# A graph layer on one core: edge features and q spans of the next pair ahead of the last node tile, span products behind the next tile, and every gather tied to one matmul

## The chip, the cores and the metric

The kernel runs on one core of a Trainium2 chip. The metric is the device time of one execution in microseconds; three executions of the kernel before took 3551.51, 3549.98 and 3547.55 us, a median of 3549.98.

A core has a matrix engine (TensorE, PE in the profile, with its weight loads shown apart as PEld), a vector engine (VectorE, DVE), a scalar engine (ScalarE, ACT), GpSimd (POOL), which here does nothing but issue gathers, and a fifth queue (SP), which here only issues transfers. Each engine works through its own queue in program order; engines wait for each other on semaphores, which an instruction raises when it ends. [...]

## The reference

One layer of message passing over 12500 nodes and 400000 edges, which are sorted by their target `dst`. All features are 32 wide, the hidden layer 64.

```python
h = jnp.maximum(_layernorm(x, axis=-1), 0.0)
...
    rol, col = (edge_index[0], edge_index[1])
    e_feat = jnp.concatenate([x[rol], x[col], edge_attr], axis=-1)
    h = jax.nn.relu(e_feat @ W1 + b1)
    v = h @ W2 + b2
    x_cand = jax.ops.segment_max(v, col, num_segments=num_nodes)
    return jnp.maximum(x_cand, x[:, -v.shape[-1]:])
x = x + _L0_gnn_ref(h, edge_index, edge_attr_32, ...)
```

Inside `_L0_gnn_ref` the argument `x` is the normalized `h`. So each edge needs the row of its source node, the row of its target node and its own 32 features; each node then takes the maximum over its edges.

## The kernel before

**Chunks.** The edges are cut into four stripes (`NS` = 4), which lie side by side on the 128 partitions, 32 features each. A stripe is cut into 196 chunks of 512 edges (`NCH`, `C`), so a chunk is 2048 edges. The main loop (L858) takes two chunks at a time, `c` and `c + 1`, and prepares the next two, `a = c + 2` and `b = c + 3`. One such pass is called an iteration here; there are 97, and the pieces under `if c:` are left out of the first.

**Layer one** adds three products into four PSUM banks `ph` (one for each stripe, the two chunks in its two halves), eight matmuls each: edge features (`edges_into`, operand `ea`), the target's part (`windows_into`; the dst order makes the targets of a chunk a short span of nodes, so `qf`, that span of the product q = h @ W1 part, is multiplied by a one-hot matrix `of`) and the source's part (`rows_into`, operand `ht`, the source rows turned so that features lie on partitions). All three go through `into_ph`, so all have line L777; they are told apart by operand. The page counts each of these matmuls as two records. ScalarE's `relu` (L802) reads the four banks into `hid`, `second_layer` (L811) multiplies by W2, and VectorE's `scan` (L819) takes the running maximum along the sorted edges.

**Source rows** come two ways. Of the 16 blocks of 128 edges in a chunk, 12 are gathered by POOL (`gather`, L181, one block of 128 rows an instruction), so 24 an iteration. The other four are picked on TensorE: `tile(c, m)` (L330) multiplies a one-hot matrix `hot` by the whole node table `hs`, held on the chip in two parts, in 14 matmuls (7 groups by 2 parts, L346); VectorE then masks the 14 candidates (`one`, L355) and reduces them to one row (`gm`, L356). A tile takes TensorE 2.9 us. In 34 chunks an extra tile `tile(b, MM)` stands for a twelfth gather (operands `hot`, `zero` and `xg` in the profile). `to_features` turns gathered rows (L372) and tile rows (L375) into `ht` on VectorE.

**Results of spans.** The iteration after, `leave_1` transposes the maxima on TensorE (L673, eight matmuls, into two banks), ScalarE and VectorE copy and split them (`so`), `leave_2` picks the last edge of each target by a matmul (L690, eight matmuls into one bank `pw`, the "span products") and copies one half on ScalarE (`wo`, L696), and `leave_3` adds the other half on VectorE (L704) and stores on SP.

**TensorE's order in one iteration**, before: edge features(c), q spans(c), rows(c), transposes, tile a1, a2, a3, second layer(c), span products, tile b0, b1, b2, b3, the extra tile where there is one, and the first tile of the chunk a + 2, called n0 below. On ScalarE the copy `wo` stands right behind the second layer, ahead of the one-hots of a + 2 (`one_hots_act`, L319 and L320).

**The order is written by hand** (`manual_schedule`): what each engine does follows the order of the Python statements, and semaphores are set where data need them. PSUM banks are handed out by `bank` from a ring of seven (`BANKS` = 7, L233): the request number k gets the bank of request k - 7 and waits for its last reader.

**Gathers held back.** A gather needs nothing but its indices and a free buffer. `HELD` holds it until a named matmul has ended: key is the gather's place among the 24, value how many iterations before the one that uses its rows, and which matmul. `passes` notes the matmuls under a name, `hold` (L220) notes the waits. Names like `a1-` and `a1` are the middle and the end of a tile, `ea`, `ht`, `tr`, `lv` the end of a group. Twenty of the 24 are held; 7, 11, 18 and 23 are not. `SOON` holds the third and fourth chunk's first ones.

## Time and profile before

| | |
|---|---|
| median of three executions | 3549.98 us |
| the profiled execution | 3553.86 us |
| its span, first to last instruction | 3552.1 us |
| mean granted TensorE clock | 0.942 of full speed |
| TensorE busy | 3301.4 us, 93% |
| VectorE, POOL, ScalarE busy | 63%, 62%, 44% |
| DMA, mean over the span | 64 GB/s |

All times in the profile are microseconds from the start of the span unless marked ns. A group in the page or in a list by lines reads: line, engine, operation, result <- operand, partitions x elements and type, count, then busy time, mean ns of one instruction, and how long the engine had been idle just before, with what ended most of that idle time ("issue" where the profile shows no reason). A timeline reads: start, duration, the same names, and in brackets the idle time ahead of the piece with what ended it; "remote" is a signal whose sender the profile doesn't tell. A windows line reads: stretch, its length, the busy time and count of PE, PEld, DVE, ACT and POOL, the granted clock, the DMA share and GB/s. Consecutive instructions of the same form stand in one line with their count.

### The profile page before, as it was taken

Reading aid. Unit: us, or ns where it says so; the run is one execution under the profiler, and the core shown is the slowest. Engines: PE = TensorE matmul, PEld = TensorE weight load, DVE = VectorE, ACT = ScalarE, POOL = GpSimd, SP = SyncE. Lnnn points to the kernel's source line nnn. Section 1 sums busy time; section 2 is a strip of 40 time slices with the busy share of each in tenths; the row PEclk is TensorE's granted clock in tenths of the full one; section 3 lists DMA queues with packets and bytes.
Section 4 is the critical chain, followed back from the end, with each engine's and each line's share of the span. In section 5 each row is a group of like instructions: output and inputs, shape, how many; then the busy total and the mean of one; then the engine's idle time right before and its main releaser. Section 6 shows DMA issues by size and latency. Waiting matters only on the chain. (4 is left out here: it accounts for less than half of the span.)

```text
span 3552.1 us, 55930 instructions
## 1 busy us (share of the span) xinstructions
PE 3301.4 (93%) x19141; PEld 2554.6 (72%) x19141; DVE 2230.3 (63%) x4215; ACT 1566.6 (44%) x2470; POOL 2208.2 (62%) x2337
## 2 busy tenths in 40 slices
PE   4799999999999999999999999999999999999997
PEld 3577777777777777777777767677767777777674
DVE  5466666666666666666666666665756666666665
ACT  4344444444444444444444444444444444444343
POOL 7566666666666666666666666666666666666662
PEclk8799999999999999999999999999999999999997
DMA  6322222212222222222222222222222222221222
GB/s 198 79 58 62 53 64 60 66 50 65 63 63 53 65 59 66 51 65 63 62 50 69 58 65 50 62 62 66 51 65 60 64 53 62 60 68 49 59 58 65
DMA packets 178823, 227.53 MB, mean 64 GB/s; under 512 B 109621, under 2 KB 150373, under 8 KB 165734
## 3 DMA queue, kind: packets, MB, share of 16 engines
q10 hardware_dynamic: 29828, 108.01, 9.5%
q0 software_dynamic: 74336, 38.21, 7.9%
q1 hardware_dynamic: 74370, 77.70, 7.2%
q8 instruction: 151, 2.47, 0.3%
q14 instruction: 138, 1.13, 0.1%
HBM read 212.23 MB, written 11.46 MB: 63 GB/s over the span
## 5 line engine op out<-in xcount | busy, mean ns | idle before, releaser
L181 POOL DMA_INDIRECT gh<-h_d,src_i x2291 | 2169.9, 947 | 1278.4 <-issue 520.4
L346 PE MATMUL pv<-hs,hot 128*128 128x448 f32 x10752 | 2319.5, 374 | 84.7 <-issue 76.9
L346 PEld LDWEIGHTS pv<-hs,hot 128*128 128x128 f32 x10752 | 2062.9, 194 | 293.5 <-issue 123.7
L355 DVE TENSOR_TENSOR one<-pv,mask 128x448 f32<-128x448 f32 x768 | 473.9, 617 | 1201.0 <-PE pv L346 569.5
L802 ACT ACTIVATE hid<-ph,wt 128x512 f32<-128x512 f32 x392 | 241.3, 688 | 1174.2 <-remote 439.0
L356 DVE TENSOR_REDUCE gm<-one 128x32 f32<-128x448 f32 x768 | 476.3, 620 | 26.5
L306 DVE TENSOR_TENSOR hot<-kb,consts 128x1024 fp32r<-128x1024 f16 (+1 forms) x379 | 447.5, 1199 | 0.0
L320 ACT ACTIVATE hot<-away,ones 128x512 fp32r<-128x512 f32 x582 | 421.8, 725 | 27.5 <-remote 8.5
L319 ACT ACTIVATE away<-kb,key_n 128x512 f32<-128x512 f16 x582 | 416.7, 716 | 0.0
L777 PE MATMUL ph<-ht,wt 32*64 32x512 f32 x1568 | 316.8, 679 | 44.6 <-issue 30.3
L696 ACT ACTIVATE wo<-pv 128x256 f32<-128x256 f32 x95 | 36.6, 385 | 673.8 <-PE pv L346 472.2
L819 DVE TENSOR_TENSOR_SCAN sm<-pb,sm,pv 128x512 f32<-128x512 bf16 x195 | 243.8, 1250 | 17.5 <-PE pv L690 6.0
L777 PEld LDWEIGHTS ph<-ht,wt 32*64 32x64 f32 x1568 | 83.3, 139 | 206.9 <-issue 178.1
L673 PEld LDWEIGHTS pv<-ident,sb 128*128 128x128 f32 x782 | 109.9, 171 | 137.9 <-issue 93.0
L372 DVE STREAM_TRANSPOSE ht<-gh 128x96 f32<-128x96 f32 x774 | 207.4, 269 | 1.2
L777 PE MATMUL ph<-of,qf 32*64 32x512 f32 x1552 | 172.8, 602 | 19.5 <-issue 16.8
L673 PE MATMUL pv<-ident,sb 128*128 128x128 f32 x782 | 150.4, 338 | 26.6 <-issue 20.5
L690 PEld LDWEIGHTS pv<-so,last 128*128 128x128 f32 x768 | 99.8, 189 | 95.6 <-issue 87.6
L665 ACT ACTIVATE sb<-sm,wt 128x512 f32<-128x512 f32 x196 | 134.3, 713 | 64.6 <-issue 41.0
L646 ACT ACTIVATE of<-of,ones 128x512 f32<-128x512 f32 x194 | 140.6, 725 | 6.3
L690 PE MATMUL pv<-so,last 128*128 128x256 f32 x768 | 126.2, 298 | 14.5 <-issue 12.9
L645 ACT ACTIVATE of<-db,below 128x512 f32<-128x512 int32 x194 | 137.4, 708 | 2.2 <-DMA db<-in_dst_ext 2.2
(115 smaller groups left out, 1330.4 us busy)
## 6 DMA issues: line engine op xcount, KB each, us to landing
ea<-in_edge_attr SPq DMA_DIRECT2D x49, 1024.0 KB
db<-in_dst_ext ACTq DMA_DIRECT2D x48, 1024.0 KB
gh<-h_d,src_i POOLq DMA_INDIRECT x2291
pb<-pen_d ACTq DMA_DIRECT2D x48, 512.0 KB
kb<-key_d ACTq DMA_DIRECT2D x47, 512.0 KB
top_d<-wo SPq DMA_DIRECT2D x752, 3.0 KB
qf<-q_d SPq DMA_DIRECT2D x392, 16.0 KB
q_d<-qs SPq DMA_DIRECT2D x6, 512.0 KB
```

The lines of the kernel that those rows point to most:

```text
L181: ins = nc.gpsimd.indirect_dma_start(out=parts[-1][:, i, :], out_offset=None, in_=h_d[:, :], in_offset=bass.IndirectOffsetOnAxis(ap=src_i[ ...
L306: nc.vector.tensor_tensor(hot_of(c)[:, start:stop], keys[c][:, None, :].to_broadcast([P, n, MM * P]), key_ps[:, start:stop, None].to_broad ...
L319: nc.scalar.activation(away, keys[c], AF.Square, bias=key_n[:, k:k + 1])
L320: nc.scalar.activation(hot_of(c)[:, k], away, AF.Relu, bias=ones, scale=-1.0)
L346: ins = nc.tensor.matmul(po, hot[k], hs[:, part, k].rearrange("p f a -> p (f a)"), start=(k == 0 and part == 0), stop=(k == A1 - 1 and par ...
L355: nc.vector.tensor_tensor(one, of_group, mask[:, None, :].to_broadcast([P, D, A0]), op=ALU.mult)
L356: nc.vector.tensor_reduce(row, one, axis=AX.X, op=ALU.max)
L673: passes(c // 2 + 1, "tr", nc.tensor.transpose(px[:, j, :], sb[:, j * P:(j + 1) * P], ident))
L690: ins = nc.tensor.matmul(pw[:, x % n], last[x][:, j].rearrange("p s w -> p (s w)"), sos[x][0][:, j], start=(j == 0 and x < n), stop=(j == ...
L777: ins = nc.tensor.matmul(ph[s][x * HID:(x + 1) * HID], w[g], e[g], start=start, stop=stop)
L802: nc.scalar.activation(hid[k], of, AF.Relu, bias=b1c)
L819: nc.vector.tensor_tensor_scan(found[:, :n], loaded.pop(c)[2][:, :n], pv[:, :n], -LOW if before is None else before[:, C - 1:C], op0=ALU.a ...
```

## The change

Four things change. `edges_into` and `windows_into` for the next pair are no longer called at the loop's top, but at the end of the iteration before, ahead of `tile(a + 2, 0)`. `leave_2`, with its copy `wo`, moves from behind `second_layer` to behind `tile(b, 0)`. `passes` gets an index, so that every single matmul of the groups can be named. `HELD` then holds all 24 gathers, each by one matmul (`b2.4` is the fifth of tile b2's fourteen).

TensorE's order after: rows(c), transposes, tile a1, a2, a3, second layer(c), tile b0, span products, tile b1, b2, b3, the extra tile, edge features(c + 2), q spans(c + 2), n0.

```diff
--- before.py
+++ after.py
@@ -64,11 +64,12 @@
 LATE = NCH - 8
 PIECE = 2 * A0
 GP = 3
-HELD = {0: (3, 'b1'), 1: (3, 'b2-'), 2: (3, 'b2'), 3: (3, 'b3-'), 4: (3, 'b3'), 5: (3, 'n0-'), 6: (3, 'n0'),
-        8: (2, 'ea'), 9: (2, 'ht'), 10: (2, 'tr'), 12: (2, 'a1-'), 13: (2, 'a1'), 14: (2, 'a2-'), 15: (2, 'a2'),
-        16: (2, 'a3-'), 17: (2, 'a3'), 19: (2, 'lv'), 20: (2, 'b0-'), 21: (2, 'b0'), 22: (2, 'b1-')}
+HELD = {0: (3, 'b1.13'), 1: (3, 'b2.4'), 2: (3, 'b2.10'), 3: (3, 'b3.3'), 4: (3, 'b3.11'), 5: (2, 'ea.0'),
+        6: (2, 'ea.7'), 7: (3, 'n0.4'), 8: (3, 'n0.12'), 9: (2, 'ht.1'), 10: (2, 'ht.7'), 11: (2, 'a1.0'),
+        12: (2, 'a1.4'), 13: (2, 'a1.9'), 14: (2, 'a2.0'), 15: (2, 'a2.8'), 16: (2, 'a3.2'), 17: (2, 'a3.9'),
+        18: (2, 'l2.0'), 19: (2, 'l2.4'), 20: (2, 'b0.6'), 21: (2, 'lv.0'), 22: (2, 'b1.0'), 23: (2, 'b1.8')}
 BANKS = 7
-SOON = {(3, 0): 'a0', (3, 6): 'a2', (4, 0): 'a3', (4, 6): 'b0', (5, 0): 'b1', (5, 6): 'b2'}
+SOON = {(3, 0): 'a0.13', (3, 6): 'a2.13', (4, 0): 'a3.13', (4, 6): 'b0.13', (5, 0): 'b1.13', (5, 6): 'b2.13'}
 ROUND = 12582912.0
 LOW = 1e30
 BY_ACT = range(A1 - 3, A1)
@@ -213,9 +214,9 @@
     gh = {}
     passed = {}
 
-    def passes(iteration, name, ins):
-
-        passed[iteration, name] = ins
+    def passes(iteration, name, ins, k):
+
+        passed[iteration, f"{name}.{k}"] = ins
 
     def hold(c, i, ins):
 
@@ -345,11 +346,9 @@
             for part in range(2):
                 ins = nc.tensor.matmul(po, hot[k], hs[:, part, k].rearrange("p f a -> p (f a)"),
                                  start=(k == 0 and part == 0), stop=(k == A1 - 1 and part == 1))
-            if k in (A1 // 2, A1 - 1):
-                at = "" if k == A1 - 1 else "-"
                 if m == 0 and c % 2 == 0:
-                    passes(c // 2 - 2, "n0" + at, ins)
-                passes(c // 2 - 1, "ab"[c % 2] + str(m) + at, ins)
+                    passes(c // 2 - 2, "n0", ins, 2 * k + part)
+                passes(c // 2 - 1, "ab"[c % 2] + str(m), ins, 2 * k + part)
         of_group = po.rearrange("p (f a) -> p f a", a=A0)
         one = early.tile([P, D, A0], F32, name="one", bufs=2)
         nc.vector.tensor_tensor(one, of_group, mask[:, None, :].to_broadcast([P, D, A0]), op=ALU.mult)
@@ -670,7 +669,8 @@
             px = bank("pv").rearrange("p (j q) -> p j q", j=J)
             n = blocks(c)
             for j in range(n):
-                passes(c // 2 + 1, "tr", nc.tensor.transpose(px[:, j, :], sb[:, j * P:(j + 1) * P], ident))
+                ins = nc.tensor.transpose(px[:, j, :], sb[:, j * P:(j + 1) * P], ident)
+                passes(c // 2 + 1, "tr", ins, c % 2 * J + j)
             so = pool.tile([P, J, 2, P], F32R, name="so", bufs=2)
             nc.scalar.activation(so[:, :n, 0], px[:, :n], AF.Copy)
             return so, px
@@ -690,7 +690,7 @@
                     ins = nc.tensor.matmul(pw[:, x % n], last[x][:, j].rearrange("p s w -> p (s w)"),
                                            sos[x][0][:, j], start=(j == 0 and x < n),
                                            stop=(j == blocks(c + x) - 1 and x >= 2 - n))
-            passes(c // 2 + 1, "lv", ins)
+                    passes(c // 2 + 1, "lv", ins, x * J + j)
             wo = pool.tile([P, 2, P], F32, name="wo", bufs=2)
             if c < NCH - 6:
                 nc.scalar.activation(wo, pw[:, :, 0], AF.Copy)
@@ -770,27 +770,27 @@
 
         sent = {}
 
-        def into_ph(ph, pairs, start, stop):
+        def into_ph(c, name, ph, pairs, start, stop):
             for s in range(NS):
                 g = slice(s * D, (s + 1) * D)
                 for x, (w, e) in enumerate(pairs):
                     ins = nc.tensor.matmul(ph[s][x * HID:(x + 1) * HID], w[g], e[g], start=start, stop=stop)
-            return ins
+                    passes(c // 2, name, ins, 2 * s + x)
 
         def edges_into(c):
 
             ph = banks[c] = [bank("ph") for s in range(NS)]
-            passes(c // 2, "ea", into_ph(ph, [(w1c, loaded[c + x][0]) for x in range(2)], True, False))
+            into_ph(c, "ea", ph, [(w1c, loaded[c + x][0]) for x in range(2)], True, False)
             return ph
 
         def windows_into(c, ph):
             of = [ofs.pop(c + x) for x in range(2)]
             q = fetched.pop(c // 2)
-            into_ph(ph, [(q[:, x], of[x]) for x in range(2)], False, False)
+            into_ph(c, "of", ph, [(q[:, x], of[x]) for x in range(2)], False, False)
 
         def rows_into(c, ph):
             ht = [hts.pop(c + x).rearrange("p k e -> p (k e)") for x in range(2)]
-            passes(c // 2, "ht", into_ph(ph, [(w1a, ht[x]) for x in range(2)], False, True))
+            into_ph(c, "ht", ph, [(w1a, ht[x]) for x in range(2)], False, True)
 
         def relu(c):
 
@@ -809,7 +809,7 @@
                 for x in range(2):
                     g = slice(x * HID, (x + 1) * HID)
                     ins = nc.tensor.matmul(pv[x][s * D:(s + 1) * D], w2x[g], hid[s][g], start=True, stop=True)
-            passes(c // 2, "l2", ins)
+                    passes(c // 2, "l2", ins, 2 * s + x)
             return pv
 
         def scan(c, pv, before):
@@ -857,9 +857,6 @@
         windows_into(0, ph)
         for c in range(0, NCH - 4, 2):
             a, b = c + 2, c + 3
-            if c:
-                ph = edges_into(c)
-                windows_into(c, ph)
             rows_into(c, ph)
             if c % LOAD:
                 load_edges(c + LOAD // 2 + AHEAD)
@@ -895,8 +892,6 @@
                 tile(a + 2, 0)
             pv = second_layer(c, hid)
             if c:
-                pw = leave_2(c - 2, so, last)
-            if c:
                 one_hots_act(a + 2)
             load_keys(a + KEYS)
             load_key_x(b + 2)
@@ -910,6 +905,7 @@
             sms = [scan(c, pv[0], sm)]
             if c:
                 tile(b, 0)
+                pw = leave_2(c - 2, so, last)
                 to_features(b, 0)
             sms.append(scan(c + 1, pv[1], sms[0]))
             sm = sms[1]
@@ -954,13 +950,11 @@
             tile(b, MM)
             to_features(b, 3)
             to_features(b, J)
+            ph = edges_into(c + 2)
+            windows_into(c + 2, ph)
             if a + 2 < NCH - 2:
                 if c:
                     tile(a + 2, 0)
-            else:
-                ph = edges_into(c + 2)
-                windows_into(c + 2, ph)
-            if a + 2 < NCH - 2:
                 to_features(a + 2, 0)
             if c == (NB - 1) * BLOCK + 2:
                 bp = bank("pv")[:, 0:1]
```

## The prediction

> **What bounds the kernel now.** I read the page's busy times and costliest groups first, then windows over single iterations, then the timeline of TensorE around two of them. The page gives TensorE as the engine that is nearly always at work:
>
> ```profile
> PE 3301.4 (93%) x19141; PEld 2554.6 (72%) x19141; DVE 2230.3 (63%) x4215; ACT 1566.6 (44%) x2470; POOL 2208.2 (62%) x2337
> ...
> L181 POOL DMA_INDIRECT gh<-h_d,src_i x2291 | 2169.9, 947 | 1278.4 <-issue 520.4
> L346 PE MATMUL pv<-hs,hot 128*128 128x448 f32 x10752 | 2319.5, 374 | 84.7 <-issue 76.9
> ```
>
> "93%" is an average over very different iterations. These windows (microseconds, busy time of PE, PEld, DVE, ACT and POOL with counts, then the granted TensorE clock) are the long middle, two neighbouring iterations counted from one second layer (L811) to the next, and inside each of them the stretch from the edge features to the next tile:
>
> ```profile
> 300.00:3400.00 3100.00, 2948.13 (x17214) 2300.76 (x17213) 1981.61 (x3753) 1379.86 (x2180) 1948.65 (x2059) 0.95 0.24 60
> 1528.60:1566.60 38.00, 36.30 (x193) 26.44 (x192) 23.25 (x46) 16.19 (x26) 23.81 (x26) 0.91 0.23 59
> 1566.60:1598.10 31.50, 31.50 (x208) 26.56 (x207) 23.97 (x46) 15.23 (x25) 20.33 (x23) 1.00 0.24 54
> ...
> 1546.57:1556.55 9.98, 9.00 (x57) 3.29 (x57) 6.57 (x15) 1.71 (x3) 6.34 (x7) 0.82 0.24 54
> 1585.58:1589.25 3.67, 3.67 (x57) 1.98 (x57) 2.65 (x5) 0.00 (x0) 1.98 (x3) 1.00 0.30 75
> ```
>
> The iteration with more matmuls (208 records, for it has an extra tile) is 6.5 us shorter, and all of that lies in the same 57 records: 9.98 against 3.67 us. The timeline says which:
>
> ```profile
> 1546.57 1.11 PE L777 MATMUL ph<-ea,wt 32*64 32x512 f32 x16
> 1547.48 1.06 PE L777 MATMUL ph<-of,qf 32*64 32x512 f32 x16
> 1548.34 1.02 PE L777 MATMUL ph<-ht,wt 32*64 32x512 f32 x2
> 1549.65 1.09 PE L777 MATMUL ph<-ht,wt 32*64 32x512 f32 x8 [0.30 <-DVE ht L375]
> 1550.98 1.01 PE L777 MATMUL ph<-ht,wt 32*64 32x512 f32 x2 [0.25 <-issue]
> 1552.43 2.57 PE L777 MATMUL ph<-ht,wt 32*64 32x512 f32 x4 [0.44 <-issue]
> 1554.93 1.97 PE L673 MATMUL pv<-ident,sb 128*128 128x128 f32 x8
> 1556.55 10.12 PE L346 MATMUL pv<-hs,hot 128*128 128x448 f32 x42
> ...
> 1582.69 2.96 PE L346 MATMUL pv<-hs,hot 128*128 128x448 f32 x14
> 1585.58 1.11 PE L777 MATMUL ph<-ea,wt 32*64 32x512 f32 x16
> 1586.49 1.13 PE L777 MATMUL ph<-of,qf 32*64 32x512 f32 x16
> 1587.34 1.13 PE L777 MATMUL ph<-ht,wt 32*64 32x512 f32 x16
> 1588.40 1.09 PE L673 MATMUL pv<-ident,sb 128*128 128x128 f32 x8
> 1589.25 8.92 PE L346 MATMUL pv<-hs,hot 128*128 128x448 f32 x42
> ...
> 1627.87 10.29 PE L346 MATMUL pv<-hs,hot 128*128 128x448 f32 x42
> ...
> 1661.37 1.05 PE L346 MATMUL pv<-hs,hot 128*128 128x448 f32 x4
> ```
>
> Edge features and q spans take 1.8 us both times. The rows (ht) take 6.6 us in one and 1.1 in the other, in pieces, between which TensorE waits first for VectorE's last transpose and then for "issue"; the granted clock falls, and the transposes and three tiles behind it take 1.97 and 10.12 instead of 1.09 and 8.92. So the bound is TensorE, with stalls at the rows and a clock that falls there; the middle's mean of 0.95 puts what the clock costs near 155 us (5% of 3100). POOL is next: a gather is 0.95 us busy and, with the row below, 0.33 of issue (520.4 over 1599), so 24 of them make 30.5 us of the 36.1 in which 24 were done (3100/2059 x 24).
>
> ```profile
> POOL gh L181 <- issue: 520.4, 1599, 3.4
> ```
>
> **The change part by part.** *1. Edge features and q spans ahead of the last tile.* TensorE does the same matmuls in another order: 1.8 us moves from behind the tile of the next window (2.9 us, row 1582.69) to ahead of it. The rows become ready a fixed time behind tile b3's end; they follow that end by the same 4.7 us either way, so their stall stays. Nothing is added on any DMA queue. What does change is the ring of seven PSUM banks, each handed out to the seventh request after it. Before, the requests run ph0 to ph3, two for the transposes, a1: the seventh back from a1 is the tile ahead of the edge features, which VectorE has long read. After, that tile's request stands between ph3 and the transposes, and the seventh back from a1 is ph0. Then **a1 cannot start before ScalarE's first relu (L802) has read ph0**; in the kernel before that relu guards a2, one tile (2.9 us) later. When it starts is in ScalarE's timeline, for the four iterations whose a1 is quoted above:
>
> ```profile
> L802 ACT ACTIVATE hid<-ph,wt 128x512 f32<-128x512 f32 x392 | 241.3, 688 | 1174.2 <-remote 439.0
> ...
> 1554.82 2.56 ACT L802 ACTIVATE hid<-ph,wt 128x512 f32<-128x512 f32 x4 [10.99 <-remote]
> ...
> 1591.07 2.42 ACT L802 ACTIVATE hid<-ph,wt 128x512 f32<-128x512 f32 x4 [12.25 <-remote]
> ...
> 1626.06 2.42 ACT L802 ACTIVATE hid<-ph,wt 128x512 f32<-128x512 f32 x4 [13.18 <-remote]
> ...
> 1662.83 2.42 ACT L802 ACTIVATE hid<-ph,wt 128x512 f32<-128x512 f32 x4 [12.73 <-PE pv L673]
> ```
>
> One relu is 0.688 us, so the first ends at 1555.51, 1591.76, 1626.75 and 1663.52, against a1 at 1556.55, 1589.25, 1627.87 and 1661.37: late by 0, 2.51, 0 and 2.15 us. It is late where the rows ran through: ph0 had its last matmul 1.2 us or less after 1587.34, yet the relu started at 1591.07, because TensorE's signals reach other engines late. The mean is 1.17 us; over the 95 iterations after the first, 111 us. That is the upper end, if every wait lengthens the span; the lower is 0, if the new marks let the signal through sooner, so that the relu is done at the transposes' end. Nothing measured favours either end, and I take the middle, **+56**. Behind a waiting a1 stand a2, a3 and the second layer; VectorE's `one` of each then is late next.
>
> *2. Span products behind tile b0.* Between the second layer and b1 TensorE's work is the same sum, so b1 to b3 end no earlier. What gains is VectorE's `one` (L355) for b0, what loses is ScalarE's copy `wo` (L696):
>
> ```profile
> 2029.39 1.22 PE L690 MATMUL pv<-so,last 128*128 128x256 f32 x8
> ...
> 2030.45 14.61 PE L346 MATMUL pv<-hs,hot 128*128 128x448 f32 x70
> ...
> 2032.79 0.39 ACT L696 ACTIVATE wo<-pv 128x256 f32<-128x256 f32 x1 [7.07 <-PE pv L346]
> ...
> 2035.78 0.62 DVE L355 TENSOR_TENSOR one<-pv,mask 128x448 f32<-128x448 f32 x1 [2.12 <-PE pv L346]
> ```
>
> The products hold TensorE for 1.06 us (2029.39 to 2030.45), and VectorE stood idle for 2.12 before b0's product, so it can start up to 1.06 us sooner, and the rows' transposes with it. Over 95 iterations that is -101 at most, where VectorE's work runs through to the rows, and 0, where it waits for b1 to b3 anyway. About every second iteration stalls at its rows, so I take half: **-50**. `wo` comes 2.9 us later, but on ScalarE the one-hots of a+2 now go ahead of it, into the 7.07 us that it idled. VectorE's sum of `wo` (L704) stands behind the second scan in both, and the stores on SP follow it. I cost this at nothing; the cover is that idle time, and if it is gone the two `of` activations behind it are late for the q spans, by the 2.9 us less 7.07, so not at all by this row.
>
> *3. Marks.* Of the 20 marks, nine sit on a matmul that signals for nothing else (the half tiles' eight and the edge features' last); of the 24 new ones, 21. So 12 signals an iteration are added: eight inside tiles, four in edge features, second layer and span products. No row shows a signal alone. The tiles' own row bounds it: 84.7 us idle over 10752 matmuls, or 768 tiles with two signals each, is 0.055 us for one if all of the idle is theirs. The second layer's matmuls, with two signals in each of 98 groups, idle 2.2 us in all, 0.011 each:
>
> ```profile
> L811 PE MATMUL pv<-hid,wt 64*32 64x512 f32 x1568 | 115.1, 606 | 2.2 <-issue 1.2 <-ACT hid L802 0.8
> ```
>
> Eight at 0.055 and four at 0.011 are 0.48 us an iteration, **+46** over 95. Bounds: 0, if they overlap the matmuls; and 12 x 0.055 x 95 = 63. [...] The four gathers that were free and now wait (7, 11, 18, 23) I cost at nothing: POOL has 36.1 less 30.5 us an iteration to spare, and a gather feeds rows two iterations on. If that cover is gone, VectorE's transposes (L372) wait for POOL, and the pace is set as in the first rival on the slow side.
>
> **Sum.** 56 - 50 + 46 = +52 us. Against the profiled execution (span 3552.1, 3553.9 with what lies around it) that is 3606; it lay 3.9 above the median of the runs, so **3602** on the median.
>
> **The rivals.** *A. The clock recovers (faster).* The sparse stretch of TensorE loses its first 1.8 us: from 9.98 to 8.2 in the stalled iteration, and a whole tile of dense matmuls comes right ahead of the rows. For: the clock was 0.82 over the 9.98 us and 1.00 over the 3.67. Against: the stall itself is 5.5 us longer than the rows' 1.1. If two thirds of the 155 us come back and the relu's wait stays small, the time is 3550 - 103 = 3447; if a third does, 3498. [...]
>
> *B. The relu's wait itself drops the clock (slower, much).* Where the rows run through, TensorE then has 1.1 of rows, 0.9 of transposes and 2.5 of waiting. If that is enough to halve the clock as in the stalled ones, whose window at 0.91 lost 3.4 of 38 us, every second iteration pays it: 48 x 3.4 = 163 on top of the 111, so 3550 + 274 = 3824; with half of it 3687. It decides from where the wait plus rows and transposes pass the 3.67 us at which the clock still stood at 1.00. POOL held by 24 waits would give the same sign: 0.25 us more for each gather makes 24 x 0.25 = 6 us, all of its slack.
>
> *C. Nothing shows.* The relu's signal comes in time, the products gain nothing and the added signals overlap: 3550.
>
> **How the numbers follow.** Forecast (3560 to 3680, the sum with its bounds: 52 with 111 for 56, nothing for -50 and 63 for 46 gives +174 at worst; 0, -101 and 0 give -101 at best; all three seldom fall together) 0.43; A 0.36; B 0.15; C 0.06. The range takes in A to 3440 and B to 3720, which leaves out the best of A and the worst of B, some 0.15 together. A measurement of this kernel tells no less than about 0.2% (7 us) from no change. A gives faster 0.36, to which the sum's low end adds 0.01; C gives same 0.06; forecast and B give slower 0.57.
>
> **What would show it.** Right: in the timeline of TensorE, a gap or a long first matmul at a1 that ends with the first relu, and more "issue" idle on the tiles' row than 84.7 us. Step 2 shows as less idle before `one` of b0; if `ht` still stalls as long, it gained nothing. A shows as a middle clock over 0.95 and fewer stretches of 10 us; B as one under 0.95, with half clock in iterations whose rows ran through. The prediction is wrong if a1 starts right behind the transposes in most iterations, or if the rows' stall changes length though their distance from b3 did not.

## The result, and the profile after

| | median, us | runs |
|---|---|---|
| before | 3551.81 | 16 |
| after | 3559.15 | 16 |

The ratio is 1.0019, with a 95% interval of 1.0010 to 1.0028: the change costs about 7 us. The profiled execution of after took 3569.83 us (span 3568.1), at the slow end of its runs (3549.18 to 3569.83). Chips differ: the kernel before takes 3004 us on two of those used below, 3552 on one and 3600 on another, within 0.5% on each, so every ratio here is against before on the same chip. (Each chip was met in one group of runs, chip 15 in two, so nothing here tells the chip from the moment.)

The page of after, its busy times, and the middle of its span as one window (columns as before):

```profile
PE 3260.8 (91%) x19141; PEld 2497.9 (70%) x19141; DVE 2226.8 (62%) x4215; ACT 1574.5 (44%) x2470; POOL 2200.6 (62%) x2337
...
300.00:3400.00 3100.00, 2891.46 (x17142) 2233.67 (x17141) 1964.07 (x3726) 1378.57 (x2167) 1933.41 (x2050) 0.97 0.23 60
```

TensorE is less busy (3260.8 against 3301.4), its clock is higher (0.97 against 0.95), and no time came of it. TensorE's groups in the list by lines say where the work got shorter and longer; line numbers move by one:

```profile
L347 PE MATMUL pv<-hs,hot 128*128 128x448 f32 x10752 | 2377.1, 376 | 92.4 <-issue 79.6 <-DVE one L354 3.6 <-DVE ht L374 1.8
...
L777 PE MATMUL ph<-of,qf 32*64 32x512 f32 x1552 | 222.6, 616 | 34.0 <-issue 29.2
L777 PE MATMUL ph<-ht,wt 32*64 32x512 f32 x1568 | 144.8, 639 | 15.2 <-issue 9.5 <-DVE ht L374 5.2
...
L690 PE MATMUL pv<-so,last 128*128 128x256 f32 x768 | 123.4, 287 | 45.2 <-issue 43.4 <-DVE ht L374 0.9
...
L321 ACT ACTIVATE hot<-away,ones 128x512 fp32r<-128x512 f32 x582 | 421.5, 724 | 330.0 <-issue 282.9 <-remote 26.1 <-ACT away L320 2.9
...
L696 ACT ACTIVATE wo<-pv 128x256 f32<-128x256 f32 x95 | 36.5, 384 | 285.3 <-PE pv L347 185.3 <-remote 64.0 <-DMA kb<-key_d 15.1
```

The rows fell from 316.8 busy and 44.6 idle to 144.8 and 15.2. The q spans grew from 172.8 and 19.5 to 222.6 and 34.0, the tiles by 58 us, and the span products idle 45 us. Busy time and idle time mix stalls and work, so here is the same from the start of each matmul to the start of the next, summed by group over 300 to 3400 us and divided by the 87 iterations that begin there (worked out from both traces, us per iteration):

```
         tiles  extra   ea    of    ht    tr   l2    lv   sum    at half clock
before   24.79  1.15  1.04  1.36  3.30  1.51  1.09  1.38  35.63  3.22
after    25.62  1.39  1.12  2.41  1.35  0.90  1.12  1.72  35.63  2.39
```

(ea, of, ht: edge features, q spans, rows; tr transposes, l2 second layer, lv span products.) Rows and transposes gain 2.56 us. Q spans, tiles, products, extra tile, edge features and second layer give back 2.57. Both sums are 3100/87, equal by the way they are made; in the 86 whole iterations of that stretch one takes 35.51 us before and 35.72 after, and the groups differ from the table by 0.1 at most. In the timeline of TensorE after, a stalled iteration looks like this:

```profile
1617.98 8.57 PE L347 MATMUL pv<-hs,hot 128*128 128x448 f32 x42
1626.48 1.11 PE L777 MATMUL ph<-ea,wt 32*64 32x512 f32 x16
1627.39 2.80 PE L777 MATMUL ph<-of,qf 32*64 32x512 f32 x9
1631.02 1.85 PE L777 MATMUL ph<-of,qf 32*64 32x512 f32 x7 [0.83 <-issue]
1632.80 4.67 PE L347 MATMUL pv<-hs,hot 128*128 128x448 f32 x14
1637.41 1.11 PE L777 MATMUL ph<-ht,wt 32*64 32x512 f32 x16
1638.45 1.09 PE L672 MATMUL pv<-ident,sb 128*128 128x128 f32 x8
1639.30 1.06 PE L347 MATMUL pv<-hs,hot 128*128 128x448 f32 x4
```

The stall has left the rows, which run through in 1.1 us, and stands at the q spans: 5.4 us from 1627.39 to 1632.80, where 1.1 is needed. The tile n0 behind it takes 4.67 us in place of 2.96, so it pays for the clock. The q spans don't wait for ScalarE: their one-hots had been written by 1624.8. What else goes on is in the timelines of ScalarE, VectorE and POOL over the same microseconds:

```profile
1624.04 0.72 ACT L645 ACTIVATE of<-of,ones 128x512 f32<-128x512 f32 x1
...
1631.83 0.62 DVE L354 TENSOR_TENSOR one<-pv,mask 128x448 f32<-128x448 f32 x1 [5.09 <-remote]
...
1614.82 0.95 POOL L182 DMA_INDIRECT gh<-h_d,src_i  x1 [0.30 <-issue]
1619.00 0.94 POOL L182 DMA_INDIRECT gh<-h_d,src_i  x1 [3.23 <-PE pv L347]
...
1628.97 0.94 POOL L182 DMA_INDIRECT gh<-h_d,src_i  x1 [0.30 <-issue]
1632.02 0.94 POOL L182 DMA_INDIRECT gh<-h_d,src_i  x1 [2.10 <-remote]
```

Nine gathers run back to back from 1619.00 to 1629.9. Tile b3 ended by 1626.5 at the latest, yet VectorE's product starts at 1631.83; POOL's next mark arrives at 1632.0; TensorE moves on at 1631.0. All three come at about one time, 2 to 3 us after the last gather of the run began. That is the theory which the experiments test: **while gathers run, TensorE's signals don't get out; its queue stalls where they pile up, and the change moves that place.** Taken to the letter it is too strong. In the middle of after (300 to 3400 us), 45% of the VectorE products that ended a wait of over 1 us began at least 2 us behind the start of the latest gather, which is so for only 7% of the time; but the other resumes came while gathers still ran (worked out from the trace).

### The profile page after: what moved, and what is told of

The parts are those of the page before. It is cut to its first block, busy times and chain, and to the rows that moved or that the text cites. A ratio compares the mean times of both kernels' runs of the same rounds, so it can differ in the third digit from the quotient of the medians.

```text
span 3568.1 us, 56072 instructions
## 1 busy us (share of the span) xinstructions
PE 3260.8 (91%) x19141; PEld 2497.9 (70%) x19141; DVE 2226.8 (62%) x4215; ACT 1574.5 (44%) x2470; POOL 2200.6 (62%) x2337
## 4 chain that ended last, share of the span: by engine, by line
PE 88%; issue 7%; DVE 3%; ACT 1%; DMA 0%; SPq 0%; POOL 0%; another core or an unknown queue 0%; DVEq 0%; POOLq 0%; ACTq 0%
PE pv L347 66%; PE ph L777 13%; PE pv L811 3%; PE pv L690 3%; PE pv L672 3%; DVE one L354 1%; DVE last L653 1%; DVE hot L307 1%; DVE sm L819 0%; DVE ht L371 0%; POOL xg L198 0%; DVE st L432 0%; SPq L628 0%; POOL gh L182 0%
## 5 line engine op out<-in xcount | busy, mean ns | idle before, releaser
L347 PE MATMUL pv<-hs,hot 128*128 128x448 f32 x10752 | 2377.1, 376 | 92.4 <-issue 79.6
L347 PEld LDWEIGHTS pv<-hs,hot 128*128 128x128 f32 x10752 | 2041.9, 193 | 471.9 <-issue 234.9
L802 ACT ACTIVATE hid<-ph,wt 128x512 f32<-128x512 f32 x392 | 242.5, 688 | 1177.9 <-PE ph L777 829.9
L777 PE MATMUL ph<-of,qf 32*64 32x512 f32 x1552 | 222.6, 616 | 34.0 <-issue 29.2
L777 PEld LDWEIGHTS ph<-of,qf 32*64 32x64 f32 x1552 | 64.5, 132 | 152.8 <-issue 149.4
L696 ACT ACTIVATE wo<-pv 128x256 f32<-128x256 f32 x95 | 36.5, 384 | 285.3 <-PE pv L347 185.3
L777 PE MATMUL ph<-ht,wt 32*64 32x512 f32 x1568 | 144.8, 639 | 15.2 <-issue 9.5
L777 PE MATMUL ph<-ea,wt 32*64 32x512 f32 x1568 | 140.7, 623 | 16.2 <-issue 15.8
L690 PEld LDWEIGHTS pv<-so,last 128*128 128x128 f32 x768 | 111.7, 191 | 54.0 <-issue 49.3
L672 PEld LDWEIGHTS pv<-ident,sb 128*128 128x128 f32 x782 | 85.6, 143 | 88.9 <-issue 48.8
```

The source lines that it names most:

```text
L347: ins = nc.tensor.matmul(po, hot[k], hs[:, part, k].rearrange("p f a -> p (f a)"), start=(k == 0 and part == 0), stop=(k == A1 - 1 and par ...
L690: ins = nc.tensor.matmul(pw[:, x % n], last[x][:, j].rearrange("p s w -> p (s w)"), sos[x][0][:, j], start=(j == 0 and x < n), stop=(j == ...
L777: ins = nc.tensor.matmul(ph[s][x * HID:(x + 1) * HID], w[g], e[g], start=start, stop=stop)
L802: nc.scalar.activation(hid[k], of, AF.Relu, bias=b1c)
```

## The experiments

All ratios are against the kernel before on the same chip, with 95% intervals. "Prompt" and "late" say how TensorE's signals arrive on that chip, as explained below the first group.

| run | spans moved | products moved | new marks | prompt: chips 4, 15 (before 3004) | late: before 3552 (chip 3) or 3600 (chip 0) |
|---|---|---|---|---|---|
| marks_only | | | x | 0.9997, 1.0004, 0.9998 | not run |
| lv_only | | x | | not run | 1.0070 (1.0057 to 1.0083), chip 3 |
| ea_only | x | | | 1.0011 (1.0002 to 1.0020) | not run |
| order_only | x | x | | 1.0019, 1.0023 | not run |
| lv_back | x | | x | 1.0007 (0.9998 to 1.0016) | not run |
| ea_back | | x | x | 0.9863 (0.9849 to 0.9877), 0.9860 | 0.9957 (0.9944 to 0.9969), chip 0 |
| after | x | x | x | 1.0027 (1.0018 to 1.0037) | 1.0019 (3), 1.0000 (0.9988 to 1.0011) (0) |

**First group, chip 4: parts of the change.** `marks_only` keeps before's order with the new `HELD` (marks of neighbouring groups put in its order). `order_only` is after with before's marks:

```diff
-HELD = {0: (3, 'b1.13'), 1: (3, 'b2.4'), 2: (3, 'b2.10'), ...
+HELD = {0: (3, 'b1.13'), 1: (3, 'b2.7'), 2: (3, 'b2.13'), ...   # before's 20
```

`lv_back` and `ea_back` are after with one of the two moves undone:

```diff
# lv_back
             pv = second_layer(c, hid)
             if c:
+                pw = leave_2(c - 2, so, last)
                 one_hots_act(a + 2)
...
                 tile(b, 0)
-                pw = leave_2(c - 2, so, last)
# ea_back
             a, b = c + 2, c + 3
+            if c:
+                ph = edges_into(c)
+                windows_into(c, ph)
             rows_into(c, ph)
```

> The order of before with the 24 new marks (those of neighbouring groups put in the order in which TensorE reaches them there). Theory S (TensorE's stall comes when gathers run back to back on POOL and its signals pile up; it appears wherever the next few signalling matmuls stand, so the parts of the change hardly matter alone): ratio to before 0.995 to 1.005, the stall again at the rows (ht idle and long pieces, as before). Theory P (two parts that cancel: the new order gained at the rows and the clock, the new marks cost it back): 1.010 to 1.020, about 40 to 70 us slower, with more issue idle on the tiles' row than 92 us.

> The changed kernel with the 20 marks of before. Theory S: ratio 0.995 to 1.005, the stall at the q spans as in the changed kernel. Theory P: 0.980 to 0.990, some 40 to 70 us faster, with the rows free as after and the tiles' idle at or below that of before (85 us).

> The changed kernel with the span products back behind the second layer (two marks swapped to follow). Theory S: within 0.5% of before, the stall still at the q spans. Theory P with the products as the part that costs (they idle 45 us after, 15 before, and ScalarE's hot waits 283 us that it did not wait before): 0.985 to 0.995. If the products are a part that gains: 1.005 to 1.015.

> The changed kernel with edge features and q spans back behind the tile n0 (marks swapped to follow). Theory S: within 0.5% of before, but the stall goes back from the q spans (2.41 us an iteration after) to the rows (3.30 before). Theory P with the moved spans as the part that gains: 1.010 to 1.025, rows over 3 us and a granted clock near 0.95 again; as the part that costs: 0.985 to 0.995.

Measured: before itself took 3003.80 us there, and none of the four traces shows the stall. The window over the middle of `marks_only`, and one iteration on its ScalarE and TensorE:

```profile
300.00:2900.00 2600.00, 2600.00 (x17038) 2128.40 (x17038) 1954.79 (x3695) 1361.44 (x2150) 1936.88 (x2050) 1.00 0.27 71
...
1513.46 1.06 PE L777 MATMUL ph<-ht,wt 32*64 32x512 f32 x16
1514.46 1.09 PE L672 MATMUL pv<-ident,sb 128*128 128x128 f32 x8
1515.31 8.90 PE L347 MATMUL pv<-hs,hot 128*128 128x448 f32 x42
...
1514.56 2.42 ACT L802 ACTIVATE hid<-ph,wt 128x512 f32<-128x512 f32 x4 [8.20 <-PE ph L777]
```

TensorE is busy for all of the 2600 us at full clock, with the same 2050 gathers. The first relu starts 1.1 us after the first row matmul (1514.56 against 1513.46); in the trace of before it took 3.7 us in an iteration whose rows ran through (1591.07 against 1587.34). The same shows over the whole middle: where VectorE was idle, its product starts 0.40 us behind the start of its tile's last matmul in `marks_only`, every time; the median is 1.9 us in before and 2.7 in after, the longest 7.7 (worked out from the traces). So on this chip the signals are prompt, and neither theory's "stall" exists to be moved. Three of the four came out within 0.3% of before, as theory S had it, but for another reason than S gave; `ea_back`, 1.4% faster, missed theory S and lies in the branch of theory P in which the moved spans are the part that costs (0.985 to 0.995).

**Second group, chip 0: gathers and holds.** `after_again` is the change itself, `ea_back_2` the kernel above. `gathers_out` leaves the gathers of chunks 9 to 193 out, `no_hold` has an empty table:

```diff
# gathers_out
+        if 8 < c < NCH - 2:
+            return gh[8]
         parts = []
# no_hold
+HELD = {}
```

> The changed kernel once more, beside the kernel before on one chip. The four runs before this showed the kernel before at 3004 us, with prompt signals from TensorE and no stall at rows or q spans. Theory C (the stalls, and with them the 3550 us, belong to the condition of the chip in which signals of TensorE arrive late while gathers run; where they arrive promptly POOL's 24 gathers of 1.25 us set the pace): where before takes about 3004, the changed kernel takes 2990 to 3020 and the clock is 0.99; where before takes about 3550, it is 3550 to 3570 as on record. Rival (the stalls belong to the two kernels with an early or late stall, and any of the four variants had cured them): 3550 or more whatever before takes.

> Same kernel as in the run of that name. Theory C with prompt signals: 0.986 again, since its marks keep POOL from waiting at all. Where before takes about 3550: within 0.5% of before, with the stall back at the rows; if it gains there as well, then the marks and the products' place help in both conditions, and the moved spans are the part of the change that costs.

> The changed kernel with the gathers of chunks 9 to 193 left out (their rows are those of chunk 8; two fewer gather buffers). Theory C: with late signals the stalls vanish with the gathers, clock 0.99, under 3000 us in place of 3560; with prompt signals TensorE's own work is left, 2850 to 2960. Rival (the stalls come from VectorE's or ScalarE's lateness, not from gathers): within 2% of the changed kernel beside it, stalls in the same places.

> The changed kernel with no gather held, so that POOL waits only for free buffers. Theory C: with late signals longer runs of gathers and longer stalls, over 3600 us; with prompt signals POOL never waits for TensorE, so 2955 to 2990, like the run ea_back. Rival (holding itself matters little): within 0.5% of the changed kernel in both.

Measured: before 3599.93; `after_again` 3601.37, ratio 1.0000; `ea_back_2` 3582.61, 0.9957; `gathers_out` 3058.72, **0.8499** (0.8485 to 0.8514); `no_hold` 4066.83, **1.1294** (1.1268 to 1.1320). The middle of `gathers_out`, then of `no_hold` as windows, and two of the waits of `no_hold` (waiting engine and line, what it waited for, us in all, times, longest):

```profile
300.00:2900.00 2600.00, 2600.00 (x16949) 2107.66 (x16948) 1951.00 (x3679) 1356.33 (x2144) 0.00 (x0) 1.00 0.18 58
```

```profile
300.00:3900.00 3600.00, 3133.64 (x17366) 2338.13 (x17365) 1996.19 (x3783) 1396.05 (x2198) 1961.71 (x2078) 0.89 0.20 52
```

```profile
POOL gh L179 <- DVE ht L368: 998.7, 283, 8.5
...
PEld pv L344 <- issue: 659.8, 710, 2.6
```

Without gathers TensorE is busy all the time at full clock and a whole iteration takes 30.3 us, as much as in the changed kernel on a prompt chip with all its gathers (30.3 in `after_fourth` below). So the stalls come with the gathers, not from VectorE or ScalarE. (The marks go with the gathers, but on the prompt chip 12 marks more an iteration cost nothing, 0.9997 in `marks_only`. The gathers' transfers are gone too, so whether POOL's issuing or the transfers do it is not told apart.) With no hold, POOL gathers until its buffers are full, TensorE's weight loads wait 660 us for "issue", and the mean clock falls to 0.89. `ea_back_2` has its stall at the rows again, 3.35 us an iteration from start to start, as expected. Theory C had the direction of `gathers_out` and `no_hold`; its figure for `gathers_out`, under 3000 us, was missed by 59, and POOL's 24 gathers don't set the pace on a prompt chip, for the loop is as long without them. Of the 46 us by which `gathers_out` is longer than `after_fourth`, 44 lie ahead of the first transposes (at 134.2 us against 89.8).

One rival stays open. In the late traces records of semaphore updates are missing in number, of VectorE too: 1601 of 3733 are there in before, against 3512 of 3544 in `marks_only`. On chip 0 it is 1479 of 3544 in `after_again` and 2729 of 2805 in `gathers_out`. So what is held up may reach beyond TensorE's signals, or lie in part in the taking of the records, and no run separates that.

**Third group, chip 3: what is left.** `bank_ahead` asks for n0's bank ahead of the four `ph` banks, meant to let a1 reuse n0's bank again. `lv_only` is before with nothing but the products moved. `groups6` has four marks, one for six gathers:

```diff
# bank_ahead
+            if c and a + 2 < NCH - 2:
+                first.append(bank("pv"))
             ph = edges_into(c + 2)
...
-        po = bank("pv")[:, :D * A0]
+        po = (first.pop() if first and m == 0 and c % 2 == 0 else bank("pv"))[:, :D * A0]
# groups6
+HELD = {0: (3, 'b1.13'), 6: (2, 'ea.7'), 12: (2, 'a1.4'), 18: (2, 'l2.0')}
```

> The changed kernel once more, on whichever chip comes. So far before took 3004 us on one chip and 3550 and 3600 on others; the changed kernel was 1.002 and 1.000 of it where before took 3550 and 3600, and hasn't been seen where it takes 3004. Theory C: 3550 to 3610 with late signals; 2990 to 3020 with prompt ones, as its parts there gave 0.9997 to 1.0019.

> The changed kernel with one edit: the bank of the tile n0 is asked for ahead of the four ph banks, so that a1 again reuses n0's bank and not the one that the first relu reads. Theory R (the relu's wait is what the moved spans cost; in the changed kernel the first relu ended on average 0.13 to 0.18 us after a1's start, 12 to 17 us in all): 0.994 to 0.998 of the changed kernel beside it. Rival (the wait costs nothing, for the stall that follows takes it up): within 0.2% of the changed kernel.

> The kernel before with the span products behind tile b0 and nothing else, so with its 20 marks. The run with products moved and new marks gave 0.9863 with prompt signals and 0.9957 with late ones; new marks alone 0.9997 with prompt ones. If the products' place is what gains: 0.985 to 0.990 with prompt signals, 0.993 to 0.998 with late ones. If it takes both: 0.998 to 1.003.

> The changed kernel with four marks in place of 24, one for each six gathers (the other five follow unheld). Theory Q (with late signals each run of gathers ends in about 1.1 us in which POOL waits for a mark, some 5.5 times an iteration, and this sets the pace; the number of runs is what counts): four runs, 0.955 to 0.985 of the changed kernel. Rival (what counts is how long a run of gathers keeps TensorE's signals back; the kernel with no holds took 1.13): over 1.01. With prompt signals 0.98 to 1.0 either way, for POOL waits less.

Measured: before 3551.55; `after_third` 3559.27, 1.0019 (1.0009 to 1.0029); `bank_ahead` 3555.13, 1.0006 (0.9993 to 1.0020); `lv_only` 3577.82, 1.0070 (1.0057 to 1.0083); `groups6` 3789.91, 1.0667 (1.0652 to 1.0682). `bank_ahead` is within 0.2% of `after_third`, as its rival had it, and three rows of after, from VectorE, TensorE and ScalarE, show that the wait which it was to remove isn't there:

```profile
3276.76 0.63 DVE L354 TENSOR_TENSOR one<-pv,mask 128x448 f32<-128x448 f32 x1 [5.29 <-PE pv L672]
...
3277.44 6.87 PE L347 MATMUL pv<-hs,hot 128*128 128x448 f32 x33 [0.85 <-DVE one L354]
...
3278.92 2.42 ACT L802 ACTIVATE hid<-ph,wt 128x512 f32<-128x512 f32 x4 [13.14 <-PE pv L347]
```

Here a1 starts right behind VectorE's product of n0, 1.5 us before the first relu of its iteration begins. In 16 of 87 iterations it starts before that relu has ended. In before, after and `bank_ahead` alike, a1's first matmuls wait for a semaphore of VectorE and a2's and a3's for one of ScalarE (in the traces' records; in before and after in 87 of 87 iterations). So the request number k does not always get the bank of request k - 7: in after a1 gets a bank that VectorE has read, n0's by these rows, and not ph0.

`groups6` overturned theory Q: fewer runs of gathers, but 6.7% slower. POOL and TensorE of it:

```profile
1512.36 0.94 POOL L179 DMA_INDIRECT gh<-h_d,src_i  x1 [2.08 <-remote]
...
1524.85 0.94 POOL L179 DMA_INDIRECT gh<-h_d,src_i  x1 [0.30 <-issue]
1531.03 0.94 POOL L179 DMA_INDIRECT gh<-h_d,src_i  x1 [5.24 <-PE pv L344]
...
1522.03 1.11 PE L687 MATMUL pv<-so,last 128*128 128x256 f32 x8
1523.71 0.36 PE L344 MATMUL pv<-hs,hot 128*128 128x448 f32 x1 [0.58 <-issue]
...
1526.54 1.09 PE L344 MATMUL pv<-hs,hot 128*128 128x448 f32 x3 [1.03 <-issue]
1527.97 8.40 PE L344 MATMUL pv<-hs,hot 128*128 128x448 f32 x36 [0.34 <-issue]
```

Eleven gathers run from 1512.36 to 1525.8. TensorE works undisturbed for the first 10 us and then creeps, one matmul at a time, until 1527.97, and the next mark reaches POOL at 1531.0. So here fewer and longer runs of gathers cost more. Runs of gathers (starts less than 1.35 us apart) are 4.1 long on average in before, 4.3 in after, 7.5 in `groups6`: 1, 1.002 and 1.067. Length alone doesn't order the kernels, though: in `no_hold` the runs are 5.3 long by the same count, and it takes 1.129.

`lv_only` lost 0.7% where a gain was expected. In its list by lines the transposes and the edge features took up what the products lost:

```profile
L671 PE MATMUL pv<-ident,sb 128*128 128x128 f32 x782 | 161.1, 335 | 68.8 <-issue 61.3 <-ACT sb L663 5.5
L776 PE MATMUL ph<-ea,wt 32*64 32x512 f32 x1568 | 156.6, 617 | 18.4 <-issue 14.9 <-DMA top_d<-wo 0.8
...
L689 PE MATMUL pv<-so,last 128*128 128x256 f32 x768 | 110.2, 284 | 6.8 <-issue 6.7
```

Transposes went from 26.6 us idle in before to 68.8, edge features from 126.1 busy and 3.9 idle to 156.6 and 18.4; the products, at 14.5 before, idle 6.8.

**Fourth and fifth group, chip 15: which parts cancel.** `ea_only` is before with nothing but the spans moved; the others repeat kernels from above.

> The order of before with the 24 new marks, where TensorE's signals come late (before at 3550 or more). The prediction's step: +46 us for 12 more signals, 1.013. Theory M (the marks gain, since they keep runs of gathers short; products alone gave 1.007 and products with new marks 0.9957): 0.985 to 0.993. Theory I (marks and products only gain together): 0.998 to 1.003.

> The changed kernel with the 20 marks of before, where signals come late. If marks gain 1.1% whatever the order: 1.010 to 1.015, since the changed kernel is 1.000 to 1.002. If the order only costs because marks and order don't fit: within 0.3% of the changed kernel.

> The kernel before with edge features and q spans ahead of the tile n0 and nothing else, so its 20 marks and the products behind the second layer. From the runs so far the spans' move on top of products and marks cost 0.5% (1.000 to 1.002 against 0.9957): if that holds alone, 1.003 to 1.008, with the stall at the q spans and the first relu no longer late at a1. The prediction's step had +56 us for it, 1.016. If freeing the rows gains where no other part stands in the way: 0.985 to 0.997.

> Products behind b0 and new marks, spans left where they were, a third time. With late signals 0.9944 to 0.9969 of before again; with prompt ones 0.985 to 0.988.

> As for the earlier run of the new marks alone: with late signals 0.985 to 0.993 if the marks gain by themselves, 0.998 to 1.003 if they gain only together with the products' place, 1.013 by the prediction's step. With prompt signals 1.000 again.

> The whole change. With late signals 1.000 to 1.002 of before, as on record. With prompt ones: 0.998 to 1.003 if the moved spans take back what products and marks gain there (0.986), 0.985 to 0.990 if they don't.

Both groups met a prompt chip, so what was expected of late signals stays untested in these six. Measured: `marks_only_2` 1.0004 (0.9995 to 1.0013), `order_only_2` 1.0023 (1.0007 to 1.0038), `ea_only` 1.0011 (1.0002 to 1.0020), `ea_back_2b` 0.9860 (0.9845 to 0.9874), `marks_only_3` 0.9998 (0.9989 to 1.0007), `after_fourth` 1.0027 (1.0018 to 1.0037). So the moved spans, on top of products and marks, cost 1.7% where signals are prompt (1.0027 against 0.9860) and 0.4% on chip 0 (1.0000 against 0.9957); alone, in `ea_only`, they cost 0.1%. A version that keeps the spans where they were, `ea_back`, beats before on all three chips on which it ran, and after on the two where both ran.

Where they are prompt, part of that cost can be read from the weight loads. After the spans, in `after_fourth` and in `ea_back` (PEld, in brackets the idle time ahead):

```profile
1516.58 0.18 PEld L777 LDWEIGHTS ph<-of,qf 32*64 32x64 f32 x8 [0.25 <-issue]
1517.57 2.77 PEld L347 LDWEIGHTS pv<-hs,hot 128*128 128x128 f32 x14 [0.81 <-DVE bad L404]
1520.64 0.23 PEld L777 LDWEIGHTS ph<-ht,wt 32*64 32x64 f32 x16 [0.30 <-issue]
1521.69 0.86 PEld L672 LDWEIGHTS pv<-ident,sb 128*128 128x128 f32 x8 [0.81 <-issue]
```

```profile
1526.87 0.18 PEld L777 LDWEIGHTS ph<-ht,wt 32*64 32x64 f32 x8 [0.25 <-issue]
1527.30 0.18 PEld L777 LDWEIGHTS ph<-ht,wt 32*64 32x64 f32 x8 [0.25 <-issue]
1528.29 0.86 PEld L672 LDWEIGHTS pv<-ident,sb 128*128 128x128 f32 x8 [0.81 <-PE ph L777]
```

With n0 between q spans and rows, TensorE changes once more an iteration from 32-row matmuls to 128-row weights, and the first such load starts after 0.81 us in which no weights were loaded. Counted in whole iterations from 300 to 2900 us, `after_fourth` takes 30.28 us for one and `ea_back` 29.70. The q spans have 0.14 of the 0.59 (0.99 against 0.86), the rows 0.05, the extra tile 0.09 and the eight tiles 0.32 (23.36 against 23.04).

Most of what the tiles have is a change of pace. Inside a tile the matmuls start 200.0 or 206.7 ns apart, and in these seven runs the pace never changes within a stretch of tiles, only from one stretch to the next (worked out from the matmuls' starts between 300 and 2900 us, TensorE at full clock throughout):

| run | a1 to a3 | b0 to b3, n0 |
|---|---|---|
| marks_only | 206.7 ns | 206.7 ns |
| ea_back | 206.7 ns | 200.0 ns |
| after_fourth, order_only, gathers_out | 200.0 ns | 206.7 ns |

In `ea_only` and `lv_back` both paces appear at every tile, about half the time each. Five tiles in place of none at the faster pace are 5 x 14 x 6.7 ns = 0.47 us, which is nearly all that `ea_back` gains on `marks_only` (29.70 against 30.18 us). Against `after_fourth` they are two tiles more, 0.19 us. What sets the pace is open. `gathers_out` has the pattern of `after_fourth` without gathers, so it isn't the gathers.

## Why the prediction was right or wrong

The forecast was 3602, +52 us, with a range of 3440 to 3720; the change cost 7 us. The sign came true by luck: the largest term of the sum is a wait that the changed kernel doesn't have, one term has the wrong sign, and the step on the rows' stall failed outright.

- **"They follow that end by the same 4.7 us either way, so their stall stays."** This is the first of two steps that failed. The stall did not belong to the rows' distance from b3; it went to the q spans (rows 3.30 to 1.35 us an iteration, q spans 1.36 to 2.41). Its cause was on a line that the prediction quoted and read as slack: POOL's gathers. "POOL is next ... 30.5 us of the 36.1" counted their time and not what they do to TensorE's signals; leaving them out takes 15% off on chip 0.
- **"a1 cannot start before ScalarE's first relu (L802) has read ph0", +56 (0 to 111).** This step failed too, and the forecast's size with it: without the term the sum is -4 us. In after, a1 starts right behind the transposes (within 0.06 us of the last one's start) in 82 of 87 iterations, which the prediction named as a sign of being wrong, and in 16 before the relu has ended, once 1.5 us before it begins (3277.44 against 3278.92). What guards a1 is VectorE, as in before. The count of seven requests was taken from `bank` and not checked against a wait in a trace. `bank_ahead`, which changes what that count would give, changed no wait of a1 and stands at 1.0006 beside 1.0019, about 4 us with overlapping intervals. The lateness itself didn't carry over either: the first relu ended 1.25 us on average after a1's start in the middle of before (early ones counted as 0), 0.13 in after, 0.00 on the prompt chips.
- **The products, -50 (-101 to 0).** The step is in the trace: VectorE's idle time ahead of b0's product fell from 1.20 to 0.40 us an iteration in the middle (worked out from the traces), but it rose from 0.09 to 1.14 ahead of b1's. The sum of it has the wrong sign where signals come late: `lv_only` took +25 us. The stall came sooner, at edge features and transposes, which was not on the list of what is late next. `wo` cost nothing that the rows show: its idle time fell from 673.8 to 285.3 us, though ScalarE's `hot` now waits 330.0 in its stead (27.5 before).
- **The marks, +46 (0 to 63).** Nothing where signals are prompt: 0.9997, 1.0004 and 0.9998 with 12 signals more an iteration; 46 us would have been 1.015. Where they come late the marks alone were not run. `ea_back` at 0.9957 against `lv_only` at 1.0070, on different chips, speaks for a gain of about 1% with the products behind b0, by argument only.
- **Rival A, the clock.** Its sign came true (0.95 to 0.97 in the middle, 3.22 to 2.39 us at half clock an iteration) and its gain did not: the q spans still take 5.4 us in the iteration shown, and the half clock now falls on n0. In the clock records of after's trace the half clock on n0 lasts from 1633.13 to 1636.54, 3.41 us, and 56 of the 60 stretches of half clock last 3.4 or 6.8 us. A lower share of half clock brought no time here, since the stall stayed and only changed its place.
- **Rival B** did not occur: the rows and transposes of after ran at half clock for 0.07 us an iteration, against 1.49 before. **Rival C** was nearest, 0.2% off, for a reason it did not name: a stall that changes its place, and edits whose effects partly cancel.

The chances had 0.57 on slower and 0.06 on no difference; a cost of 0.19% lies at the boundary between them. What stays open: why TensorE's signals wait for gathers on some chips and not on others, what the new marks and the moved spans do alone where they wait, and so which edits make up the 7 us there.

## What to carry to other kernels

When a stall ends with "issue" and several engines resume in the same microsecond, look for what ended just before on an engine that seems idle enough, and test it by leaving its work out; here, moving the stalled work only moved the stall. Before a wait becomes a term, find one instance of it in a trace: something that starts right behind what it is said to wait for, and never ahead of it. A lateness measured in one order is not a property of the instruction (the first relu's was 1.25 us in before and 0.13 in after), so don't carry it into another order either. And compare on one chip: here a kernel differs by 20% between chips (3004 to 3600 us), far more than the change, and a variant that gains 1.4% on one gains 0.4% on another.

## What was not expected of the hardware

- The same kernel takes 3004 us on chips 4 and 15, 3552 on chip 3 and 3600 on chip 0, each within 0.5% over 17 runs or more. A gather takes the same time in all (944 to 947 ns mean); what differs is when TensorE's signals reach the others (VectorE's products 0.40 us behind their last matmul's start on chip 4, 1.9 in the median of before at 3552).
- On the late chip 0 the 24 gathers an iteration cost 15% of the whole time (0.8499 without them); POOL, which issues them, is 62% busy in the page of after. With fewer holds they cost more: 1.067 with four marks (chip 3), 1.129 with none (chip 0).
- On a prompt chip the run `ea_back` keeps POOL gathering almost without a break (208 gathers in a run on average, 300 to 2900 us) and TensorE busy throughout the middle at full clock, and takes 2963 us.
- At full clock the same tile matmuls run at one of two paces, 200.0 or 206.7 ns from start to start, and keep it until other matmuls come between (no stretch of tiles in the seven runs above mixes them): five tiles of eight at the faster one are most of the 1.4% by which `ea_back` is shorter than `marks_only` on chip 4.
